# A deformable bottleneck and a batch-normalised bottleneck: table rows of two neighbours instead of four, and the last statistics taken from the product itself

## The chip, the cores and the metric

The kernel runs on one core of a Trainium2 chip. The metric is the device time of one execution in microseconds (us), on the only core used. Matrix products run on PE, its weight loads are shown as PEld; DVE, ACT and POOL are the vector, scalar and GpSimd engines; SP issues transfers. ACT and POOL issue transfers too, in the same order in which they do their other work.

## The reference, cut to what matters

Two layers follow each other on x of 4 images, 1024 channels, 56 x 56 pixels, all in float32. CB is 256.

```python
# layer 0
r = relu(conv1x1(x, w1) + b1)                      # 1024 -> 256
off = conv3x3(r, w_off) + b_off                    # 2 offsets for each of 9 taps and pixel
ys, xs = pixel + tap + off
y0, x0 = floor(ys), floor(xs); wy1, wx1 = ys - y0, xs - x0
sampled = ( r[y0, x0]     * (1-wy1)*(1-wx1) + r[y0, x0 + 1]     * (1-wy1)*wx1
          + r[y0 + 1, x0] * wy1*(1-wx1)     + r[y0 + 1, x0 + 1] * wy1*wx1 )   # 0 outside the image
r = relu(einsum('nckhw,ock->nohw', sampled, w2) + b2)
x1 = relu(x + conv1x1(r, w3) + b3)                 # 256 -> 1024
# layer 1
o = relu(bn(conv1x1(x1, w1) + b1))                 # bn: mean and variance over images and pixels
o = relu(bn(conv3x3(o, w2) + b2))
o = bn(conv1x1(o, w3) + b3)                        # 256 -> 1024
out = relu(x1 + softplus(residual_scale) * o)
```

Every bn needs the mean and the variance of a whole product, over all 4 x 3136 pixels, before one value of it can be scaled.

## The kernel before

Channels lie on the 128 partitions, so 1024 channels are 8 groups (KC) and 256 are 2 (KB). Pixels are worked in blocks of 8 image rows, 448 pixels: 7 blocks (NJ) an image, 28 in all. A float32 product of 128 x 448 is issued to PE as two instructions.

**The deformable layer.** stage_a (one block of an image) loads x (SP, L207), makes the 1x1 product (L211), ReLU to feat (ACT, L220), the offset product (L230), and turns feat by PE transposes (L254) into rows of one pixel each, ft (ACT, L260 to L263). ACT then writes ft to a table in device memory, one table for each image (L267, L271). A table row stands for one pixel of the image with a border of zeros, 58 pixels to a row (PW). It holds 256 channels for each of four neighbours: the pixel, its right neighbour, the one below, and the one below right. So every block is written four times, each time shifted, with two DMAs (384 KB and 80 KB): eight in all. The border is written with zeros at the start (L189). stage_b makes four weights for each pixel and tap and the row to read (L297 to L319).

stage_c takes a block of the image before. For each of the 9 taps, sampled fetches 4 tiles of 112 pixels: POOL gathers 112 table rows of 4 KB (L332) into one of 8 buffers g, ACT scales the first neighbour (L340), DVE adds the other three (L342), PE turns the sum (L351), and ACT copies two finished halves to sts (L357). The products with w2 (L369) run one tap behind. Then come ReLU (L385), the product with w3 (L408), the sum with x (DVE, L415), ReLU (L418), the store of x1 to device memory (L422), and layer 1's first product (L391) with its statistics (L426, L429).

What sets the order: the outer loop calls stage_a of image n, stage_b of the block before and stage_c of image n - 1, for each j. So the first 7 blocks have only stage_a, the last 7 only stage_c. Each engine works in the order of its own instruction list; a tile scheduler fixes that list when the program is built, from the program's order and its own estimate of times. On ACT the eight table writes of stage_a stand directly ahead of the two copies to sts with which the next block of stage_c begins (L357).

**Layer 1.** c2w and c3w are loaded, the first bn is applied on the way into padded images (L494), the 3x3 convolution runs (L515), its result stays in SBUF as y2, with its statistics (L524, L525).

**The last statistics.** The last product is z = c3w x y2, of 1024 channels. Its mean follows from the mean of y2, and its variance from the second moments of y2, a 256 x 256 matrix. So y2 is normalised (ACT, L594), turned to pixel rows by PE (L564), a reference value of each channel is subtracted (DVE, L578), POOL sets a column of ones (L571), and PE multiplies each chunk of 128 pixels with itself (moments, L583). At the end gram x c3w (L641), a product with c3w element by element (L644) and sums over channels on PE (L651) give mean and variance (L658 to L661), and scale_shift_of gives scale and shift.

**The last product.** Function wide makes one 128 x 448 piece of z in one of 4 PSUM banks (L533). DVE scales it and adds x1 (L675), ACT does shift and ReLU (L683), and the result is stored (L686). x1 comes back from device memory into 4 buffers x1f (SP, L672).

Of the kernel before, what the change touches and what calls it, by code (L numbers as in the profile page):

```python
# [8 lines left out]
F32 = mybir.dt.float32  # L9
I32 = mybir.dt.int32  # L10
AF = mybir.ActivationFunctionType
ALU = mybir.AluOpType

N, CIN, H, W = 4, 1024, 56, 56
CB = 256
# [31 lines left out]
def deform_bottleneck_then_bn_bottleneck(  # L47
# [30 lines left out]

    tables = [
        dram.tile([TROWS, 4, CB], F32, tag=f"table{n}", name=f"table{n}") for n in range(N)  # L80
# [18 lines left out]
    y2_stats = const.tile([128, KB, NB, 6], F32, tag="y2_stats", name="y2_stats")  # L99

    def scale_shift(stats, k, g, be, name):

        mv = const.tile([128, k, 2], F32, tag=f"mv_{name}", name=f"mv_{name}")
        for i in range(k):
            nc.vector.bn_aggr(mv[:, i, :], stats[:, i, :, :].rearrange("p b s -> p (b s)"))
        return scale_shift_of(mv[:, :, 0], mv[:, :, 1], k, g, be, name)

    def scale_shift_of(mean, var, k, g, be, name, bias=None):

        sc = const.tile([128, k], F32, tag=f"sc_{name}", name=f"sc_{name}")  # L110
        sh = const.tile([128, k], F32, tag=f"sh_{name}", name=f"sh_{name}")
        nc.scalar.activation(sc, var, AF.Sqrt, bias=eps_t)
        nc.vector.reciprocal(sc, sc)
        nc.vector.tensor_mul(sc, sc, g)
        if bias is None:
            nc.vector.tensor_mul(sh, mean, sc)
            nc.vector.tensor_sub(sh, be, sh)
        else:
            nc.vector.tensor_add(sh, mean, bias)
            nc.vector.tensor_sub(sh, bias, sh)  # L120
            nc.vector.tensor_mul(sh, sh, sc)
            nc.vector.tensor_add(sh, sh, be)
        return sc, sh


    with ExitStack() as l0:
# [57 lines left out]
        for n in range(N):  # L184
            for corner, s in enumerate((0, 1, PW, PW + 1)):
# [15 lines left out]
        def stage_a(n, j):  # L201
# [63 lines left out]
            for corner, s in enumerate((0, 1, PW, PW + 1)):  # L265
# [9 lines left out]
        def stage_b(n, j):  # L275
# [37 lines left out]
            for corner in range(4):  # L313
                wy, wx = (hi if corner // 2 else lo), (hi if corner % 2 else lo)
# [228 lines left out]


    stat = ctx.enter_context(tc.tile_pool(name="stat", bufs=1))
    gram = stat.tile([128, KB, KB, 128], F32, tag="gram", name="gram")
    dev = stat.tile([128, KB], F32, tag="dev", name="dev")
    ref = stat.tile([128, KB], F32, tag="ref", name="ref")
    ref_all = stat.tile([128, CB], F32, tag="ref_all", name="ref_all")
    part = stat.tile([128, 128], F32, tag="part", name="part")  # L550
    nc.vector.memset(part, 1.0 / 128)
    prod = stat.tile([128, KB, CIN], F32, tag="prod", name="prod")
    mom = stat.tile([128, 3, KC], F32, tag="mom", name="mom")
    chunks = [(n, at, min(128, HW - at)) for n in range(N) for at in range(0, HW, 128)]
    with ExitStack() as l2:
        pixp = l2.enter_context(tc.tile_pool(name="pixels", bufs=3))
        acc_g = ps2.tile([128, KB, 512], F32, tag="acc", name="acc_g")

        def pixels(i):

            tp = ps1.tile([128, 2, CB], F32, tag="bank", name=f"tp_{i}")
            for c, (n, at, m) in enumerate(chunks[i : i + 2]):
                for h in range(KB):
                    nc.tensor.transpose(  # L564
                        tp[:m, c, h * 128 : (h + 1) * 128], y2[n][:, h, at : at + m], ident
                    )
            yt = pixp.tile([128, 2, CB + 1], F32, tag="ytp", name=f"ytp_{i}")
            return tp, yt

        def centred(i, tp, yt):  # L570
            nc.gpsimd.memset(yt[:, :, CB : CB + 1], 1.0)  # L571
            ms = [m for _, _, m in chunks[i : i + 2]]
            for c in range(2) if min(ms) < 128 else (slice(0, 2),):
                m = ms[c] if isinstance(c, int) else 128
                of = ref_all if isinstance(c, int) else (
                    ref_all.rearrange("p (o c) -> p o c", o=1).to_broadcast([128, 2, CB])
                )
                nc.vector.tensor_tensor(yt[:m, c, :CB], tp[:m, c, :], of[:m], ALU.subtract)  # L578

        def moments(i, yt):  # L580
            for c, (n, at, m) in enumerate(chunks[i : i + 2]):
                for h in range(KB):
                    nc.tensor.matmul(  # L583
                        acc_g[:, h, : CB + 1 - h * 128],
                        yt[:m, c, h * 128 : (h + 1) * 128],
                        yt[:m, c, h * 128 :],
                        start=(i == 0 and c == 0),
                        stop=(i + c == len(chunks) - 1),
                    )

        def relu(n, j):
# [5 lines left out]

        done = 0
        before = None
        for i in range(0, len(chunks), 2):  # L600
            n, at, m = chunks[i + 1]
            while done * BLK < n * HW + at + m:
                relu(done // NJ, done % NJ)
                done += 1
            tp, yt = pixels(i)
            if i == 0:
                nc.vector.tensor_copy(yt[:, 0, :CB], tp[:, 0, :])
                first = ps1.tile([128, 512], F32, tag="bank", name="first")
                nc.tensor.matmul(first[:, :CB], part, yt[:, 0, :CB], start=True, stop=True)
                nc.vector.tensor_copy(ref_all, first[:, :CB])  # L610
                first_c = ps1.tile([128, 512], F32, tag="bank", name="first_c")
                for h in range(KB):
                    nc.tensor.matmul(
                        first_c[:, h : h + 1],
                        yt[:, 0, h * 128 : (h + 1) * 128],
                        part[:, 0:1],
                        start=True,
                        stop=True,
                    )
                nc.vector.tensor_copy(ref, first_c[:, :KB])  # L620
            centred(i, tp, yt)
            if before is not None:
                moments(*before)
            before = (i, yt)
        moments(*before)

        total = float(N * HW)
        nc.vector.tensor_scalar_mul(gram[:, 0], acc_g[:, 0, :CB].rearrange("p (b c) -> p b c", c=128), 1.0 / total)
        nc.vector.tensor_scalar_mul(gram[:, 1, 1], acc_g[:, 1, :128], 1.0 / total)
        nc.vector.tensor_scalar_mul(dev[:, 0:1], acc_g[:, 0, CB : CB + 1], 1.0 / total)  # L630
        nc.vector.tensor_scalar_mul(dev[:, 1:2], acc_g[:, 1, 128:129], 1.0 / total)
        nc.vector.tensor_add(ref, ref, dev)
        mirror = ps1.tile([128, 512], F32, tag="bank", name="mirror")
        nc.tensor.transpose(mirror[:, :128], gram[:, 0, 1], ident)
        nc.vector.tensor_copy(gram[:, 1, 0], mirror[:, :128])
        for h in range(KB):
            for half in range(2):
                pg = ps1.tile([128, 512], F32, tag="bank", name=f"pg_{h}_{half}")
                cs = slice(half * 512, (half + 1) * 512)
                for g in range(KB):  # L640
                    nc.tensor.matmul(  # L641
                        pg, gram[:, g, h], c3w[:, g, cs], start=(g == 0), stop=(g == KB - 1)
                    )
                nc.vector.tensor_mul(prod[:, h, cs], pg, c3w[:, h, cs])  # L644
        pm3 = ps1.tile([128, 3, KC], F32, tag="bank", name="pm3")
        nc.vector.memset(part[:, 0:1], 1.0)
        for k in range(KC):
            ks = slice(k * 128, (k + 1) * 128)
            for what, (of, by) in enumerate(((c3w, ref), (c3w, dev), (prod, None))):
                for h in range(KB):  # L650
                    nc.tensor.matmul(  # L651
                        pm3[:, what, k : k + 1],
                        of[:, h, ks],
                        part[:, 0:1] if by is None else by[:, h : h + 1],
                        start=(h == 0),
                        stop=(h == KB - 1),
                    )
        nc.vector.tensor_copy(mom, pm3)  # L658
        nc.vector.tensor_mul(mom[:, 1], mom[:, 1], mom[:, 1])
        nc.vector.tensor_sub(mom[:, 2], mom[:, 2], mom[:, 1])  # L660
        nc.vector.tensor_scalar_max(mom[:, 2], mom[:, 2], 0.0)  # L661
    sc3, sh3 = scale_shift_of(
        mom[:, 0], mom[:, 2], KC, cols("g3", KC), cols("be3", KC), "bn3", bias=cols("b3", KC)
    )
# [75 lines left out]
```

## Time and profile before

| | |
|---|---|
| time, median of 3 runs | 4442.2 us (4433.05 to 4461.87) |
| the profiled execution | 4433.05 us, of which the span is 4431.3 us |
| mean granted PE clock | 0.927 |
| PE busy | 3732.4 us (84%) |
| weight loads | 1918.2 us (43%) |
| DVE busy | 1907.6 us (43%) |
| ACT busy | 1237.1 us (28%) |
| POOL busy | 1119.7 us (25%) |
| gathers L332 | 1008, from issue to landing 10.4 us (median) |
| last gather issued | 3140.9 us |
| 3x3 convolution L515 | from 3203.5 us, for 759.6 us |
| first transpose of the moments L564 | 3968.5 us |
| last product L533 | 896 instructions, the first at 4078.2 us, the last at 4424.5 us |
| read from device memory, written | 638.65 MB, 169.79 MB |

How to read the profile: the span runs from the first to the last instruction of the profiled execution. Busy shares are means over stages of a very different kind, so most of what follows reads stretches of the span instead. In a time-ordered line the columns are start, duration, engine, line, operation, output and input with their shapes, count, and in brackets the idle time of the engine just before, with what ended it. An engine's name with a q (ACTq, SPq) marks the issuing of a transfer. A wait is listed as engine, tile and line, then what it waited for, total time, times, and the longest.

### The profile page before, as it was taken

The page shows a single profiled execution, that of the slowest core. Times are in us where ns is not written, and L with a number is a line of the kernel's source. Part 1 is how long each engine was busy: PE and PEld are TensorE (multiplying, and loading weights), DVE is VectorE, ACT ScalarE, POOL GpSimd, SP SyncE. Part 2 cuts the span into 40 slices and gives each one's busy share as a digit, 9 for nine tenths or more (in the row PEclk, how much of TensorE's full clock was granted, in tenths as well). Part 3 has the DMA queues.
Part 4 walks back from the last instruction along what each step waited for, and adds up shares of the span by engine and source line. Part 5 has one row for each costly group of instructions (what it writes and reads, how often), then busy time and mean ns, then how long its engine had stood idle before and what let it go on. Part 6 is the DMA issues. An engine that isn't in the chain of part 4 may idle for free. (4 is left out here: it accounts for less than half of the span.)

```text
span 4431.3 us, 35493 instructions
## 1 busy us (share of the span) xinstructions
PE 3732.4 (84%) x11135; PEld 1918.2 (43%) x11135; DVE 1907.6 (43%) x4208; ACT 1237.1 (28%) x2390; POOL 1119.7 (25%) x1067
## 2 busy tenths in 40 slices
PE   7887887778878878778887777787699999999999
PEld 3443344334443434333443333343355555558554
DVE  1355555545555545555555565655500000013444
ACT  0133333233332333333333333333310000021444
POOL 0233333333333333333333344443200000000000
PEclk9899998889998989999899889899899999999999
DMA  6787788888777887777877778888610000000998
GB/s 204 226 222 214 215 212 221 218 219 221 221 221 209 229 206 222 221 216 221 217 221 212 204 212 221 234 230 225 196 51 17 13 0 0 0 17 9 306 303 296
DMA packets 357149, 810.82 MB, mean 183 GB/s; under 512 B 30128, under 2 KB 243040, under 8 KB 356448
## 3 DMA queue, kind: packets, MB, share of 16 engines
q0 software_dynamic: 129024, 462.49, 40.7%
q1 hardware_dynamic: 102864, 176.25, 13.4%
q10 hardware_dynamic: 125072, 169.82, 10.9%
q8 instruction: 88, 1.44, 0.1%
q14 instruction: 101, 0.83, 0.1%
HBM read 638.65 MB, written 169.79 MB: 182 GB/s over the span
## 5 line engine op out<-in xcount | busy, mean ns | idle before, releaser
L332 POOL DMA_INDIRECT g<-table,idxs x1008 | 1112.4, 1104 | 2026.4 <-DVE s L342 1507.2
L342 DVE SCALAR_TENSOR_TENSOR s<-g,wts,s 112x256 f32<-112x256 f32 x3024 | 1364.9, 483 | 506.5 <-ACT s L340 454.2
L369 PE MATMUL acc<-sts,w 128*128 128x448 f32 x2016 | 1080.5, 656 | 404.8 <-ACT sts L357 404.8
L515 PE MATMUL acc<-pad,c2w 128*128 128x448 f32 x2016 | 759.5, 539 | 19.4 <-ACT pad L494 19.4
L340 ACT ACTIVATE s<-g,wts 112x256 f32<-112x256 f32 x1008 | 500.2, 509 | 923.5 <-DMA g<-table,idxs 671.5
L369 PEld LDWEIGHTS acc<-sts,w 128*128 128x128 f32 x2016 | 399.6, 226 | 643.8 <-ACT sts L357 483.9
L515 PEld LDWEIGHTS acc<-pad,c2w 128*128 128x128 f32 x2016 | 381.4, 189 | 397.5 <-issue 397.5
L351 PEld LDWEIGHTS stp<-ident,s 112*128 112x128 f32 x2016 | 269.0, 155 | 553.9 <-DVE s L342 344.6
L351 PE MATMUL stp<-ident,s 112*128 112x112 f32 x2016 | 369.9, 286 | 163.4 <-DVE s L342 157.7
L391 PE MATMUL acc<-x1t,c1w 128*128 128x448 f32 x896 | 381.1, 552 | 32.0 <-ACT x1t L418 31.9
L408 PE MATMUL pr<-r,w 128*128 128x448 f32 x896 | 376.5, 548 | 20.5 <-ACT r L385 20.5
L211 PE MATMUL acc<-xt,w 128*128 128x448 f32 x896 | 349.3, 547 | 29.6 <-DMA xt<-in_x_dram 29.6
L415 DVE SCALAR_TENSOR_TENSOR x1t<-pr,ch,xr 128x448 f32<-128x448 f32 x224 | 151.4, 682 | 458.2 <-PE pr L408 322.6
L533 PE MATMUL pf<-y,c3w 128*128 128x448 f32 x896 | 339.5, 542 | 0.0
L525 DVE BATCH_NORM_STATS2 y_stats<-y 128x6 f32<-128x448 f32 x56 | 32.3, 618 | 691.0 <-ACT y L524 691.0
L357 ACT COPY sts<-stp 128x448 f32<-128x448 f32 x504 | 243.0, 532 | 203.3 <-DMA table<-ft 107.0
L418 ACT ACTIVATE x1t<-x1t 128x448 f32<-128x448 f32 x224 | 129.1, 576 | 528.8 <-DVE x1t L415 502.7
L391 PEld LDWEIGHTS acc<-x1t,c1w 128*128 128x128 f32 x896 | 166.8, 191 | 214.7 <-issue 147.2
L408 PEld LDWEIGHTS pr<-r,w 128*128 128x128 f32 x896 | 170.9, 193 | 202.3 <-issue 133.7
L211 PEld LDWEIGHTS acc<-xt,w 128*128 128x128 f32 x896 | 170.9, 192 | 194.0 <-issue 184.7
L533 PEld LDWEIGHTS pf<-y,c3w 128*128 128x128 f32 x896 | 171.0, 191 | 166.5 <-issue 143.6
L242 DVE COPY offc<-pm 32x448 f32<-32x448 f32 (+1 forms) x84 | 51.4, 612 | 440.4 <-PE pm L230 439.6
(120 smaller groups left out, 1281.7 us busy)
## 6 DMA issues: line engine op xcount, KB each, us to landing
xt<-in_x_dram SPq DMA_DIRECT2D x112, 448.0 KB
xr<-in_x_dram SPq DMA_DIRECT2D x112, 448.0 KB
x_d<-x1t ACTq DMA_DIRECT2D x112, 448.0 KB
x1f<-x_d SPq DMA_DIRECT2D x112, 448.0 KB
out_dram<-x1f ACTq DMA_DIRECT2D x112, 448.0 KB
table<-ft ACTq DMA_DIRECT2D x112, 384.0 KB
g<-table,idxs POOLq DMA_INDIRECT x1008, 10.4
y_d<-y ACTq DMA_DIRECT2D x28, 448.0 KB
```

The source lines that it names most:

```text
L211: nc.tensor.matmul(acc[:, h, :BLK], w1[:, k, h * 128 : (h + 1) * 128], xt[:, d, :], start=(k == 0), stop=(k == KC - 1),)
L332: nc.gpsimd.indirect_dma_start(out=g, out_offset=None, in_=tables[n].rearrange("r q c -> r (q c)"), in_offset=bass.IndirectOffsetOnAxis(ap ...
L340: nc.scalar.activation(s, g[:, 0:CB], AF.Copy, scale=wt[:, 0])
L342: nc.vector.scalar_tensor_tensor(s, g[:, corner * CB : (corner + 1) * CB], wt[:, corner], s, ALU.mult, ALU.add,)
L351: nc.tensor.transpose(banks[h][:, t * PIX : (t + 1) * PIX], s[:, h * 128 : (h + 1) * 128], ident[:PIX, :PIX],)
L357: nc.scalar.copy(sts[:, h, :], banks[h])
L369: nc.tensor.matmul(acc[:, o, :BLK], w2[:, h, k, o * 128 : (o + 1) * 128], sts[:, h, :], start=(k == 0 and h == 0), stop=(k == TAPS - 1 and ...
L391: nc.tensor.matmul(acc3[:, h, :BLK], c1w[:, k, h * 128 : (h + 1) * 128], x1t, start=(k == 0), stop=(k == KC - 1),)
L408: nc.tensor.matmul(pr, w3[:, h, k * 128 : (k + 1) * 128], r2[:, h, :], start=(h == 0), stop=(h == KB - 1),)
L415: nc.vector.scalar_tensor_tensor(x1t[:, d, :], pr, col("a_b3", k), xr[:, d, :], ALU.add, ALU.add)
L515: nc.tensor.matmul(acc[:, o, :BLK], c2w[:, h, t, o * 128 : (o + 1) * 128], pads[n % 2][:, h, r0 : r0 + ROWS, kj : kj + W], start=(h == 0 a ...
L533: nc.tensor.matmul(pz, c3w[:, h, k * 128 : (k + 1) * 128], y2[n][:, h, j * BLK : (j + 1) * BLK], start=(h == 0), stop=(h == KB - 1),)
```

## The change

It has two parts.

Tables: a row holds two neighbours, the pixel and the one below, so it is 2 KB instead of 4 KB. The gather still fetches 4 KB for each pixel: a row and the next one, which is that of the right neighbour. The four values arrive as pixel, below, right, below right, so the weights of the second and third are exchanged. A block is written twice instead of four times, with four DMAs instead of eight; the border takes 12 DMAs instead of 24.

Statistics: the moments, their pool and their tiles are gone. In their place the whole last product is computed once more ahead of time, only for its statistics: for each block y2 is normalised, and bn_stats reads each of the 8 pieces from PSUM. scale_shift aggregates them (8 channel groups of 28 blocks) and takes over the branch with a bias.

```diff
     tables = [
-        dram.tile([TROWS, 4, CB], F32, tag=f"table{n}", name=f"table{n}") for n in range(N)
+        dram.tile([TROWS, 2, CB], F32, tag=f"table{n}", name=f"table{n}") for n in range(N)
     ]
...
+    z_stats = const.tile([128, KC, NB, 6], F32, tag="z_stats", name="z_stats")
+
+    def scale_shift(stats, k, g, be, name, bias=None):
-    def scale_shift(stats, k, g, be, name):
         mv = const.tile([128, k, 2], F32, tag=f"mv_{name}", name=f"mv_{name}")
         for i in range(k):
             nc.vector.bn_aggr(mv[:, i, :], stats[:, i, :, :].rearrange("p b s -> p (b s)"))
-        return scale_shift_of(mv[:, :, 0], mv[:, :, 1], k, g, be, name)
-
-    def scale_shift_of(mean, var, k, g, be, name, bias=None):
+        mean, var = mv[:, :, 0], mv[:, :, 1]
...
-            for corner, s in enumerate((0, 1, PW, PW + 1)):
+            for corner, s in enumerate((0, PW)):
                 first_row = PW - s + TPAD
...
-            for corner, s in enumerate((0, 1, PW, PW + 1)):
+            for corner, s in enumerate((0, PW)):
                 r = q - s + TPAD
...
-                wy, wx = (hi if corner // 2 else lo), (hi if corner % 2 else lo)
+                wy, wx = (hi if corner % 2 else lo), (hi if corner // 2 else lo)
...
-    stat = ctx.enter_context(tc.tile_pool(name="stat", bufs=1))
...
-        for i in range(0, len(chunks), 2):
-            n, at, m = chunks[i + 1]
-            while done * BLK < n * HW + at + m:
-                relu(done // NJ, done % NJ)
-                done += 1
-            tp, yt = pixels(i)
...
-            centred(i, tp, yt)
-            if before is not None:
-                moments(*before)
-            before = (i, yt)
-        moments(*before)
...
-    sc3, sh3 = scale_shift_of(
-        mom[:, 0], mom[:, 2], KC, cols("g3", KC), cols("be3", KC), "bn3", bias=cols("b3", KC)
+    for n in range(N):
+        for j in range(NJ):
             for h in range(KB):
                 ys = y2[n][:, h, j * BLK : (j + 1) * BLK]
                 nc.scalar.activation(
                     ys, ys, AF.Relu, bias=sh2[:, h : h + 1], scale=sc2[:, h : h + 1]
                 )
+            for k in range(KC):
+                nc.vector.bn_stats(z_stats[:, k, n * NJ + j, :], wide(n, j, k, "pz"))
+    sc3, sh3 = scale_shift(
+        z_stats, KC, cols("g3", KC), cols("be3", KC), "bn3", bias=cols("b3", KC)
     )
```

The gather itself, which no line of the diff shows, asks for a g tile of 4 x CB values from the table seen as rows of 2 x CB.

More of the change, by code (lines that the diff above doesn't have):

```diff
@@ L540, in wide @@
         return pz
-    stat = ctx.enter_context(tc.tile_pool(name="stat", bufs=1))
[L546 to L591, printed above, removed]
@@ L596, in relu @@
                 )
-        done = 0
-        before = None
-        for i in range(0, len(chunks), 2):
-            n, at, m = chunks[i + 1]
-            while done * BLK < n * HW + at + m:
-                relu(done // NJ, done % NJ)
-                done += 1
-            tp, yt = pixels(i)
[L606 to L620, printed above, removed]
-            centred(i, tp, yt)
-            if before is not None:
-                moments(*before)
-            before = (i, yt)
@@ L625, in deform_bottleneck_then_bn_bottleneck @@
-        moments(*before)
[L627 to L661, printed above, removed]
-    sc3, sh3 = scale_shift_of(
-        mom[:, 0], mom[:, 2], KC, cols("g3", KC), cols("be3", KC), "bn3", bias=cols("b3", KC)
+            for k in range(KC):
+                nc.vector.bn_stats(z_stats[:, k, n * NJ + j, :], wide(n, j, k, "pz"))
+    sc3, sh3 = scale_shift(
+        z_stats, KC, cols("g3", KC), cols("be3", KC), "bn3", bias=cols("b3", KC)
```

## The prediction

> **What bounds the kernel now.** I read four views of the profile, in this order. First the span in 40 slices, to find the stages:
>
> ```profile
> PE   7887887778878878778887777787699999999999
> DVE  1355555545555545555555565655500000013444
> DMA  6787788888777887777877778888610000000998
> GB/s 204 226 222 214 215 212 221 218 219 221 221 221 209 229 206 222 221 216 221 217 221 212 204 212 221 234 230 225 196 51 17 13 0 0 0 17 9 306 303 296
> ```
>
> A slice is 110.8 us. Up to about 3195 us (slice 29) no engine is full: PE 70 to 80%, DVE about 55%, DMA about 80%. That is the deformable layer, blocks of gathers. After it PE alone is full. Second, busy time by stretches of the late part:
>
> ```profile
> 3195.00:3968.00 773.00, 759.55 (x2016) 381.42 (x2016) 47.67 (x78) 77.17 (x119) 0.17 (x3) 0.99 0.05 17
> 3968.00:4062.80 94.80, 93.10 (x608) 85.61 (x609) 36.53 (x62) 36.28 (x56) 4.78 (x47) 0.97 0.02 7
> 4062.80:4088.00 25.20, 25.20 (x116) 20.55 (x115) 3.17 (x7) 0.00 (x0) 0.00 (x0) 0.71 0.00 1
> 4088.00:4431.00 343.00, 337.40 (x894) 170.19 (x894) 150.18 (x236) 145.91 (x225) 0.00 (x0) 0.99 0.89 295
> ```
>
> Columns: length, then busy time and count of PE, weight loads, DVE, ACT and POOL, granted clock, DMA share, GB/s. The 3x3 convolution, the statistics (second and third row: what the change removes) and the last product follow one another with PE full, the products at a clock of 0.99. What PE gains or loses there is span. Third, the chain of work, which gives PE's true rate, since the durations of pipelined matmuls overlap:
>
> ```profile
> 3203.47 759.56 PE acc L515 x2016
> 4087.91 325.48 PE pf L533 x862
> ```
>
> 759.56/2016 = 0.3768 us and 325.48/862 = 0.3776 us for each of the two instructions that one 128x448 product becomes. Fourth, time-ordered lines of ACT and POOL around a block's start, and the waits:
>
> ```profile
> 1099.68 0.38 ACT L263 COPY ft<-ftp 80x256 f32<-80x256 f32 x1
> 1099.83 0.37 ACTq L267 DMA_DIRECT2D table<-ft  x1
> 1100.29 0.44 ACTq L271 DMA_DIRECT2D table<-ft  x1
> ...
> 1104.78 0.54 ACTq L271 DMA_DIRECT2D table<-ft  x1
> 1105.36 0.97 ACT L357 COPY sts<-stp 128x448 f32<-128x448 f32 x2 [5.30 <-DMA table<-ft]
> ```
>
> ```profile
> 1058.88 0.93 POOL L332 DMA_INDIRECT g<-table,idxs  x1 [1.95 <-ACT x1t L418]
> 1109.59 1.23 POOL L332 DMA_INDIRECT g<-table,idxs  x1 [49.78 <-DVE s L342]
> 1111.13 6.42 POOL L332 DMA_INDIRECT g<-table,idxs  x1 [0.31 <-DVE s L342]
> ```
>
> ```profile
> ACT sts L357 <- DMA table<-ft: 107.0, 21, 9.7
> ```
>
> A block (about 112 us) has two halves. For some 62 us (59 to 66 by POOL's lines of all blocks) 36 gathers run, most of the time with the DMA engines full (share 1.03 from 1010 to 1070) at 1.73 us a gather. Then POOL stands for 50 us: all 8 g buffers are full, and PE does the 1x1 products and the next image's first products. That half ends only when ACT has issued eight table writes and at last copies sts: 5.3 us of waiting, 107.0 us in the 21 blocks that have such writes.
>
> [...]
>
> **The change, part by part.**
>
> Removed, the moments: PE's first transpose at 3968.49 to the last product of pm (L651) at 4087.78, 119.3 us, in which one pf product (2 x 0.378 = 0.8 us) was already done: 118.5 us.
>
> Added, the product twice: 4 images x 7 blocks x 8 output groups x 2 = 448 products, 896 instructions x 0.3776 = 338.3 us, and 0.6 us at its start, because ACT normalises the second half of y2 0.64 us after the first (first transposes at 3968.49 and 3969.13). 338.9 us. What runs beside it: two Relu of 0.746 us per 12.1 us on ACT, and 224 bn_stats from PSUM. The trace has bn_stats only from SBUF (L525, 618 ns);[...] an estimate of 0.68 us, as the scalar_tensor_tensor from PSUM (L675, 682 ns). Bounds: 0.62 and, a tenth above L675, 0.75. Against 1.51 us of PE per output group all of these hide behind PE, 4 banks deep; uncovered they would be 152 us.
>
> Its end: in DVE's order each bn_aggr of the last block stands behind its own bn_stats, so one aggregate (875 ns) and 1.9 us for root, reciprocal and scales follow the last statistics: 0.68 + 0.88 + 1.9 + the first STT's 0.68 = 4.1 us. PE meanwhile fills four banks with pf, 4 x 1.51 = 6.0 us: no stall. Statistics: 338.9 - 118.5 = **+220.4 us**.
>
> The x1f loads are issued when the convolution ends, and only four fit: nothing changes for them.
>
> Table writes: per block of stage_a 4 DMAs in place of 8 on ACT's queue, and 0.95 MB instead of 1.9 MB (26.6 MB less in all). The rows of L267 and L271 give 4.96 to 5.10 us from the first issue to the last's end in 18 of the 20 blocks behind the first, and 2.07 to 2.12 us for the first four: 2.9 us less on ACT, the end of which releases sts, taps, the next ACT scalings, DVE and POOL's first gather. The product that sts copies is there at about 1101.0, the fourth issue ends near 1101.9: ACT is still last, so the whole 2.9 us counts. 20 x 2.9 = 58 us. In the first block the eight take 9.87 us, four 1.93; the transpose (195.95) is then last and 7 us come off. Sum **-65 us**.
>
> The bytes: they go out in POOL's pause. In blocks of the last image, with no table writes, the first gather (2737.61) also lands 12.0 us later (ACT at 2749.64), as at 1109.59 to 1121.59. So writes have drained when gathers start; fewer bytes are worth 0, at most 1 us a block (20 us).
>
> Zero borders: 12 issues instead of 24, at the very start. They hold ACT to 42.26 us, but PE then waits for xt until 39.64 and does six matmuls before it needs feat: 0, at most 5 us.
>
> The gathers: same 1008 instructions, same 4 KB per row (in order: pixel, the one below, then both for the right neighbour; swapped weights cost nothing). The trace of before has no read at 2 KB pitch, where neighbouring rows share half their bytes. Spacing there ranges from 1.44 to 1.95 us by block[...]. I take no change, bounds of -4% and +4% on 28 x 62 = 1740 us: 70 us either way. If a row became two packets, the upper end.
>
> Orders: PE issues the four products of the first tap in one go instead of two by two, as it does already in the last image: nothing.
>
> Sum: 4431.3 + 220.4 - 65 = 4586.7 us of span, 1.8 us around it: 4588.5, against 4433.05 of the profiled execution. That run is the fastest of the three; the median lies 9 us above. I put 4593, halfway.
>
> **The rivals.** (a) The ACT time saved is given back: gathers start 2.9 us sooner, but the DMA engines or DVE take it up. For it: the gather half is DMA-bound. Against: its length hardly depends on when it starts (62 us with the long pause, 63 without stage_a). 4593 + 65 = 4658.
> (b) The new rows gather worse: two packets, or two engines on the same bytes at once. For it: gathers reach 265 GB/s where xt loads reached 413 (30 to 35 us). 5% of 1740 us: 4680.
> (c) Not slower: shared rows make memory easier, and gathers run down to DVE's three passes, 3 x 0.483 = 1.45 us. Four blocks already show 1.44 to 1.49. Over the 26 steady gathers of the other 24 blocks: 0.28 x 26 x 24 = 175 us, 4418. It decides from 0.15 us a gather on all 28 blocks (109 us), where the time comes within 1% of before. Against: the engines show a share of 1.03 throughout, and bytes per gather are the same.
> (d) Half of (c), 4510.
>
> **How the numbers follow.** Forecast 0.64, (a) 0.10, (b) 0.14, (c) 0.05, (d) 0.07. The forecast's own range is 4560 to 4625; to hold 8 in 10 it reaches towards (a) and (d): 4530 to 4660. About 1% is what a measurement can tell from no change. Only (c), with stronger gains than its sum, is faster; (c) and a strong (d) are within 1%: 0.02 and 0.04; slower 0.94.
>
> **What would show it.** Right: 896 pz instructions in 338 us with DVE about 45% busy; pf without a pause behind them; the wait of sts on table writes near 45 us instead of 107; gather spacing as before; blocks some 2.9 us shorter. Wrong: a gather packet count that doubles, spacing off by more than 0.1 us, PE waiting on bn_stats, or a lower clock in 1440 us of dense PE.

## The result and the profile after

The kernel after takes 4578.3 us (median of 4 runs, 4572.8 to 4602.5), the kernel before, on the same chip, 4446.4 us (4 runs, 4433.1 to 4461.9): a ratio of 1.031 with a 95% interval of 1.026 to 1.036. Slower, by 132 us. The forecast was 4593.

The profiled execution of after took 4572.81 us, its span is 4571.0 us: 139.7 us more than the 4431.3 us of before. On both sides it is the fastest execution. First the span in slices, of 114.3 us now:

```profile
PE   8888777888888888887787777778999999999999
DVE  1555555555555555555556656661000000444444
```

The deformable layer ends in slice 27. The slices in which PE is full are now twelve, and in the last six of them DVE is at four tenths: three slices of the new pass, three of the last product. The chain of work that ended last (start, length, what) and the stretch of the new pass (columns as in the prediction) give lengths and loads:

```profile
3122.42 760.66 PE acc L515 x2016
...
3888.53 338.86 PE pz L533 x896
4227.39 318.72 PE pf L533 x848
```

```profile
3885.00:4229.00 344.00, 340.47 (x901) 172.09 (x902) 150.43 (x238) 37.46 (x58) 0.00 (x0) 0.99 0.01 5
```

The pass takes 338.86 us at a granted clock of 0.99, with DVE busy 150 of 344 us. The convolution starts 81.05 us earlier than before (3203.47). What stands between the two kernels, by groups of instructions (busy and mean ns, then the idle time ahead of them and what ended it):

```profile
L533 PE MATMUL pz<-y,c3w 128*128 128x448 f32 x896 | 338.9, 541 | 5.5 <-ACT y L547 5.5
L533 PE MATMUL pf<-y,c3w 128*128 128x448 f32 x896 | 336.9, 539 | 0.0
L551 DVE BATCH_NORM_STATS2 z_stats<-pz 128x6 f32<-128x448 f32 x224 | 141.5, 632 | 192.8 <-PE pz L533 192.8
L357 ACT COPY sts<-stp 128x448 f32<-128x448 f32 x504 | 243.2, 532 | 161.6 <-PE stp L351 149.6 <-issue 5.8 <-DMA table<-ft 4.8
```

PE never waits for bn_stats in pz, and pf has no pause in front of it. DVE waits for PE instead (192.8 us). The wait of sts on table writes, 107.0 us before, is 4.8 and that on PE's transposes has grown from 94.9 to 149.6. Part of this is a change of name only, as the start of one block of after shows. ACT and then POOL at the start of one block of after:

```profile
955.05 0.38 ACT L263 COPY ft<-ftp 80x256 f32<-80x256 f32 x1
955.19 0.37 ACTq L267 DMA_DIRECT2D table<-ft  x1
...
956.62 0.56 ACTq L271 DMA_DIRECT2D table<-ft  x1
957.22 0.97 ACT L357 COPY sts<-stp 128x448 f32<-128x448 f32 x2 [1.80 <-issue]
```

```profile
961.45 1.23 POOL L332 DMA_INDIRECT g<-table,idxs  x1 [46.31 <-DVE s L342]
```

Four issues take 1.99 us (955.19 to 957.18), where eight took about 5. sts starts 0.04 us behind the last of them, so it still waits for them, 1.80 us here and in most of the blocks. Behind the first block that holds in 17 of 20 blocks; in the other three the transposes end last. The profile names PE for it in 16 of the 20, and "issue" or the table write in the others, because the transposes end only about 1 us earlier. And POOL's idle time is 46.3 us, where the block shown of before had 49.8. The queues (packets, MB, share), before and then after:

```profile
q0 software_dynamic: 129024, 462.49, 40.7%
...
q10 hardware_dynamic: 125072, 169.82, 10.9%
```

```profile
q0 software_dynamic: 129024, 462.49, 38.9%
...
q10 hardware_dynamic: 96808, 142.72, 8.6%
```

q0, the gathers, has exactly the packets and bytes of before: with overlapping 4 KB reads they are 129024 packets as with rows of their own. q10 holds the table writes.

Where the 139.7 us come from, and what the prediction had for each (profiled executions, us; a pause runs from a block's last gather to the next block's first; "the first pf" is the one from which the pf products run on without a break):

| | before | after | difference | predicted |
|---|---|---|---|---|
| first gather issued | 177.2 | 156.3 | -20.9 | 0 to -5 |
| first block's 48 gathers | 89.7 | 82.1 | -7.6 | -7 |
| 20 pauses with table writes, mean | 50.47 | 47.54 | 20 x -2.93 = -58.6 | -58 |
| 7 other pauses, mean | 28.82 | 27.47 | 7 x -1.35 = -9.4 | 0 |
| gathers of blocks 1 to 20, mean | 62.16 | 63.17 | 20 x 1.01 = +20.2 | 0, bounds 70 |
| the rest up to the convolution (6 blocks and the last) | | | -4.7 | 0 |
| convolution starts | 3203.5 | 3122.4 | -81.0 | -65 |
| convolution L515 | 759.6 | 760.7 | +1.1 | 0 |
| its end to the first pf | 124.9 | 344.3 | +219.4 | +220.4 |
| first pf to the end | 343.4 | 343.6 | +0.2 | 0 |

The first row was the surprise. ACT's lines at the very start, before and then after:

```profile
1.19 40.99 ACTq L189 DMA_DIRECT2D table<-zero  x24
42.26 1.28 ACT L220 ACT_TABLE_LOAD   x1 [42.26 <-DMA table<-zero]
```

```profile
1.19 16.28 ACTq L189 DMA_DIRECT2D table<-zero  x12
17.56 1.28 ACT L220 ACT_TABLE_LOAD   x1 [17.56 <-DMA table<-zero]
```

and PE's, before and after:

```profile
17.52 8.42 PE L211 MATMUL acc<-xt,w 128*128 128x448 f32 x16 [17.52 <-DMA xt<-in_x_dram]
27.18 6.28 PE L211 MATMUL acc<-xt,w 128*128 128x448 f32 x16 [1.24 <-DMA xt<-in_x_dram]
39.64 4.85 PE L211 MATMUL acc<-xt,w 128*128 128x448 f32 x6 [6.18 <-DMA xt<-in_x_dram]
```

```profile
19.95 17.02 PE L211 MATMUL acc<-xt,w 128*128 128x448 f32 x38 [19.95 <-DMA xt<-in_x_dram]
```

In before PE has to wait for xt again and again while the zero writes are out; in after it waits once. Up to 180 us these waits come to 29.6 us in before and 19.9 in after, so they hold about half of the 20.9 us; how the rest comes about was not followed. The prediction read these two facts side by side (ACT held to 42 us, PE late for xt) and took them for independent.

### The profile page after: what moved, and what is told of

Its sections match the earlier page's. It is cut to its first block, busy times and chain, and to the rows that moved or that the text cites. A ratio compares the mean times of both kernels' runs of the same rounds, so it can differ in the third digit from the quotient of the medians.

```text
span 4571.0 us, 35698 instructions
## 1 busy us (share of the span) xinstructions
PE 3944.2 (86%) x11312; PEld 1983.0 (43%) x11312; DVE 2013.2 (44%) x4367; ACT 1236.9 (27%) x2390; POOL 1140.7 (25%) x1017
## 3 DMA queue, kind: packets, MB, share of 16 engines
q0 software_dynamic: 129024, 462.49, 38.9%
## 5 line engine op out<-in xcount | busy, mean ns | idle before, releaser
L332 POOL DMA_INDIRECT g<-table,idxs x1008 | 1138.3, 1129 | 1921.5 <-DVE s L342 1422.3
L515 PE MATMUL acc<-pad,c2w 128*128 128x448 f32 x2016 | 760.6, 539 | 19.1 <-ACT pad L494 19.1
L515 PEld LDWEIGHTS acc<-pad,c2w 128*128 128x128 f32 x2016 | 381.8, 189 | 397.9 <-issue 397.7
L211 PE MATMUL acc<-xt,w 128*128 128x448 f32 x896 | 345.7, 543 | 19.9 <-DMA xt<-in_x_dram 19.9
L525 DVE BATCH_NORM_STATS2 y_stats<-y 128x6 f32<-128x448 f32 x56 | 32.3, 618 | 718.2 <-ACT y L524 718.2
L533 PE MATMUL pz<-y,c3w 128*128 128x448 f32 x896 | 338.9, 541 | 5.5 <-ACT y L547 5.5
L357 ACT COPY sts<-stp 128x448 f32<-128x448 f32 x504 | 243.2, 532 | 161.6 <-PE stp L351 149.6
L533 PEld LDWEIGHTS pz<-y,c3w 128*128 128x128 f32 x896 | 171.0, 191 | 173.4 <-issue 166.6
```

The lines of the kernel that those rows point to most:

```text
L211: nc.tensor.matmul(acc[:, h, :BLK], w1[:, k, h * 128 : (h + 1) * 128], xt[:, d, :], start=(k == 0), stop=(k == KC - 1),)
L332: nc.gpsimd.indirect_dma_start(out=g, out_offset=None, in_=tables[n].rearrange("r q c -> r (q c)"), in_offset=bass.IndirectOffsetOnAxis(ap ...
L357: nc.scalar.copy(sts[:, h, :], banks[h])
L515: nc.tensor.matmul(acc[:, o, :BLK], c2w[:, h, t, o * 128 : (o + 1) * 128], pads[n % 2][:, h, r0 : r0 + ROWS, kj : kj + W], start=(h == 0 a ...
L533: nc.tensor.matmul(pz, c3w[:, h, k * 128 : (k + 1) * 128], y2[n][:, h, j * BLK : (j + 1) * BLK], start=(h == 0), stop=(h == KB - 1),)
```

## The experiments

Twelve runs, each set beside runs of the kernel before on the same chip.

**The two parts alone.** stats_alone is after with the tables of before; tables_alone is before with this edit:

```diff
-        dram.tile([TROWS, 4, CB], ...
+        dram.tile([TROWS, 2, CB], ...
-            for corner, s in enumerate((0, 1, PW, PW + 1)):      # L185 and L265
+            for corner, s in enumerate((0, PW)):
-                wy, wx = (hi if corner // 2 else lo), (hi if corner % 2 else lo)
+                wy, wx = (hi if corner % 2 else lo), (hi if corner // 2 else lo)
```

> Only the statistics are changed; the table keeps four neighbours. If the two parts add up, as the sum of the prediction takes it, this costs 219 us: about 4446 + 219 = 4665 us, the first product of the convolution starts near 3203 us as before, and the pz stage lasts 339 us. If the two parts help or hinder each other (for example through a clock that falls in the longer dense stretch), it differs from that by more than 15 us.

> Only the tables are changed; the moments stay. Theory: -81 us, as between the two starts of the convolution (3203.5 and 3122.4), of which 21 us before the first gather, 8 us in the first block, and some 50 us from 20 pauses that are 3 us shorter, less what the gathers vary: about 4365 us. Rival: gathers of overlapping rows are slower or faster in themselves: then the 28 gather halves differ from 62.4 us in the mean by more than 1.5 us. A version that is faster than both kernels if the theory holds.

Measured: tables_alone 4388.0 us, ratio 0.988 (0.980 to 0.995), -63 us; first gather 156.4, pauses 48.01, gathers of a block 62.98 and the convolution at 3138.7. That is the table part as predicted (-65), though by other terms: the pauses gave 49 of the 58 us, the start 21 where 0 to 5 stood. The -81 of its own expectation is missed by 18 us; the interval, about -88 to -22 us, holds both. stats_alone 4621.7 us, ratio 1.041 (1.036 to 1.045): +171, not +219. In its profile the pass is as long as in after, and the missing time lies ahead of the convolution, which starts at 3135.4 although nothing of that part was edited. (The profiled execution is the fastest of its four, 31 us under their median, so 68 us is too much for a typical one.) The sum of the parts, 108 us, is 24 less than the 132 us of the whole. The statistics are taken up again below.

**What the zero writes did.** before_zero64 is before with zero writes of 64 rows, 24 as before, with more bytes (rows beyond the border are overwritten later by the tables' own writes):

```diff
-        zero = wp.tile([PW + 2, CB], ...
+        zero = wp.tile([64, CB], ...
+                        r0, r1 = (0, 64) if r0 == 0 else (TROWS - 64, TROWS)
```

> The kernel before, with each zero write widened from 59, 58 or 1 row to 64 rows (rows of the image that it covers are written over later). Theory: the start is held by zero writes that run on one or two of the 16 DMA engines[...]. Then the 24 issues end near 8 us instead of 42, the first xt no longer wait, and the first gather comes 20 to 28 us earlier, with more bytes and as many issues: about 4423 us. Rival: the number of issues or the bytes hold the start: no gain, or a loss of some us.

Measured: 4425.7 us, 0.996 (0.994 to 0.998), first gather at 159.2 instead of 177.2. Twice as many issues as after and more bytes, yet nearly all of after's earlier start. In the profiled execution only 7 of these 18 us are left when the convolution starts (3196.7): the gathers take longer (94.7 us in the first block, 89.7 in before). ACT's line at the start of before_zero64:

```profile
1.19 18.00 ACTq L190 DMA_DIRECT2D table<-zero  x24
```

The mean busy share of the DMA engines in 40 slices of the first 45 us, before and then before_zero64:

```profile
DMA  0149931162149771000189611999999700011110
```

```profile
DMA  0178999787999798968999999999999999726999
```

No run here shows the DMA engines one by one, but the shares fit zero writes that keep very few of them busy. By the times of its own packets q10, the queue of the zero writes, took 5.9% of the time of 16 engines from 1.19 to 42.18 us in before, which is 0.94 of one engine's time, an estimate from that share. From 18.0 to 21.4 us q10 takes 6.3%, all else 1.1%, and the share of both is 0.07 at 27 GB/s; from 36.0 to 39.5 us, where PE stands idle because an xt load has not landed, it is 0.06 at 23 GB/s. In before_zero64 no slice from 2.25 to 39.4 us is under six tenths, with as many issues and 1536 KB instead of 944. So the one or two engines of the expectation fit before; that the number of rows sets how many was the author's assumption and was not shown. After has four of each of these writes instead of eight; before_zero64 shows that the start it gains needs no change of the tables.

**ACT's issuing or the bytes.** before_sp is before with `nc.sync` in place of `nc.scalar` at L267 and L271. tables_eight is tables_alone with each of the four writes cut in two:

```diff
+                for t0, t1 in ((0, 1), (1, QFULL)):
                     nc.scalar.dma_start(
-                    tables[n][r : r + QFULL * 128, ...], ft[:, :QFULL, :]
+                    tables[n][r + t0 * 128 : r + t1 * 128, ...], ft[:, t0:t1, :]
...
+                for p0, p1 in ((0, 48), (48, QREST)):
```

> The kernel before, with the table writes issued by SP instead of ACT: the same eight DMAs and bytes. Theory: what the table change saves in each block is ACT's time to issue, so here the copy to sts comes about 4 us earlier than before (transposes are then last), and 21 blocks give 80 to 90 us: about 4360 us. Rival: the bytes of the table writes hold the gathers: no gain. Between them: gathers start earlier but into writes that are still under way, and half of it is lost.

> The new tables with the statistics of before, and each of the four table writes of a block cut in two, so that eight are issued again with half the bytes. Theory that the issuing on ACT is what the blocks gained: the eight take near 5 us again, a pause lasts near 50.5 us as before, and only the earlier start (21 us) is left of the gain of tables_alone: near 4425. Rival, that the bytes are: a pause stays near 48 us and the time near that of tables_alone, 4388.

Measured: before_sp 4323.4 us, 0.972 (0.968 to 0.975): -127.6 with all eight writes and all bytes, twice the gain of tables_alone and more than the 80 to 90 us of the expectation. Two views of one of its blocks, ACT and SP:

```profile
1055.51 0.38 ACT L263 COPY ft<-ftp 80x256 f32<-80x256 f32 x1
1056.14 0.53 ACT L357 COPY sts<-stp 128x448 f32<-128x448 f32 x1 [0.25 <-PE stp L351]
```

```profile
1055.65 0.37 SPq L267 DMA_DIRECT2D table<-ft  x1
...
1060.09 0.52 SPq L271 DMA_DIRECT2D table<-ft  x1
```

The same issues take 5.0 us on SP, and sts no longer waits for them: it starts 0.25 us after ft, where in before it waited 4.8 to 5.4. tables_eight gave 4377.2 us, 0.985 (0.980 to 0.990), on the side of the bytes rather than of the issues. But it had not doubled ACT's issue time: the eight smaller issues took 3.48 us a block, not 5, and by its interval it is not told from tables_alone, so it does not decide. Put in order of the time that ACT spends on issues per block (sum of their durations over 28), the pauses follow it:

| | bytes | issues | ACT issuing, us a block | mean pause |
|---|---|---|---|---|
| before | all | 8 | 4.98 | 50.47 |
| stats_again (below) | all | 8 | 4.30 | 49.37 |
| tables_eight | half | 8 | 3.48 | 48.88 |
| tables_alone | half | 4 | 1.97 | 48.01 |
| after | half | 4 | 1.86 | 47.54 |
| before_sp | all | 8 | 0 | 44.58 |
| tables_zero64_sp (below) | half | 4 | 0 | 44.71 |

The last two rows settle it for the pause: with the issues off ACT, half the bytes are worth nothing (44.71 against 44.58). The last kernel has the wider zero writes too; the new tables with SP and nothing else were not run. 5.9 us of the pause went with 5.0 us of issuing. Not all of the 5.9 is shown to be ACT's: the seven pauses without table writes are 1.2 us shorter in before_sp too (28.82 and 27.63), and why was not found.

**DVE in the new pass.** stats_twice is after with each of its bn_stats done twice from the same bank:

```diff
-                nc.vector.bn_stats(z_stats[:, k, n * NJ + j, :], wide(n, j, k, "pz"))
+                pz = wide(n, j, k, "pz")
+                nc.vector.bn_stats(z_twice[:, k, n * NJ + j, :], pz)
+                nc.vector.bn_stats(z_stats[:, k, n * NJ + j, :], pz)
```

> The kernel after with every bn_stats of the last product done twice from the same PSUM bank. Theory that PE alone sets the length of the new pass: 2 x 0.632 = 1.26 us of DVE for a group stays under the 1.51 us of PE, nothing is added but one bn_stats at the end (under 2 us), near 4580. Rival, that DVE's reading of the banks holds PE: any wait of PE for DVE shows, and the pass grows by up to 141 us, to 4720 at most.

Measured: 4574.8 us, 1.030 (1.025 to 1.036), after's own ratio.

```profile
L534 PE MATMUL pz<-y,c3w 128*128 128x448 f32 x896 | 338.6, 541 | 5.5 <-ACT y L548 5.5
L534 PE MATMUL pf<-y,c3w 128*128 128x448 f32 x896 | 337.4, 539 | 1.3 <-DVE x1f L568 1.3
L553 DVE BATCH_NORM_STATS2 z_twice<-pz 128x6 f32<-128x448 f32 x224 | 141.0, 630 | 77.9 <-PE pz L534 77.9
```

137 us more of DVE's work cost PE nothing in pz and 1.3 us at its end. PE sets the length of the pass, with 1.24 us of DVE's work beside 1.51 us of PE's for a group.

**Both savings at once.** tables_zero64_sp has tables_alone's edit, before_zero64's and before_sp's.

> The new tables with the statistics of before, the zero writes of 64 rows instead of 58 or 59, and the table writes issued from SP instead of ACT. If the three savings come from one resource, ACT's time in issuing, they do not add up: near 4300, that is before_sp (4323) less the earlier start (some 20 us), and nothing for two instead of four copies of a block. If the bytes or the number of writes count by themselves, it goes to near 4255, that is 63 us more below before_sp.

Measured: 4315.3 us, 0.971 (0.967 to 0.976), the ratio of before_sp and 15 us above the lower gain of the expectation. The savings don't add up. The first gather comes 28 us earlier than before_sp's (148.3 against 176.3), but the first block's gathers then take 88.7 instead of 78.2, and the convolution starts only 11 us earlier.

**Why the statistics cost 171 and not 219.** before_shift is before with one unused tile where after has z_stats:

```diff
+    unused = const.tile([128, KC, NB, 6], F32, ...)
+    nc.vector.memset(unused, 0.0)
```

> The kernel before with one unused constant tile of 128 x 1344 float32 (5.4 KB a partition, set to zero once) where the new statistics have z_stats, so that everything allocated after it in SBUF lies as in the kernel after; nothing else changes. Theory that the place in SBUF is what shortened the gather part of stats_alone: the convolution starts some 50 to 68 us earlier, near 3140 us, and the time is near 4400. Rival, that stats_alone differed for another reason (its executions spread from 4591 to 4638): the time stays within 10 of the kernel before, near 4450, and the convolution starts near 3203.

Measured: 4444.7 us, 1.000 (0.997 to 1.002), convolution at 3213.3. The place in SBUF is not it. Then the kernel of stats_alone once more (stats_again), and before with the new pass beside its moments (the same loop with bn_stats, ahead of L664's scale_shift_of):

> The same kernel as stats_alone, placed on the chip anew. If what shortened its gather part (convolution at 3135 us instead of 3203) was chance of that run, it now takes the kernel before plus 219, near 4660, with the convolution near 3203 and eight table writes issued in 4.65 us. If it belongs to the program, it takes near 4620 again, with the eight issued in 4.00 us.

> The kernel before, with its moments, and the new pass with its bn_stats after them, whose statistics are not used. The work up to the convolution is that of the kernel before. If removing the moments is what shortens the gather part, this kernel has none of it: the convolution starts near 3203 us, eight table writes are issued in 4.65 us, and the time is the kernel before plus the pass of 339: near 4785. If having the new pass is what shortens it, the convolution starts near 3140 us and the time is near 4735.

Measured: stats_again 4639.3 us against 4468.3, 1.040 (1.036 to 1.044), the ratio of stats_alone; convolution at 3179.4. pass_and_moments 4800.8 us, 1.077 (1.071 to 1.082), +332, convolution at 3235.0. So the shortening is not chance and goes with taking the moments out. Its size varies: the same kernel's convolution started at 3135.4 and at 3179.4. ACT's issues showed one part of a way: in a block of stats_again

```profile
985.08 0.46 ACTq L267 DMA_DIRECT2D table<-ft  x1
...
986.16 0.45 ACTq L267 DMA_DIRECT2D table<-ft  x1
```

the third and fifth issue take 0.46 and 0.45 us, where in a block of before the same two take 0.57 and 0.81:

```profile
990.73 0.57 ACTq L267 DMA_DIRECT2D table<-ft  x1
...
991.91 0.81 ACTq L267 DMA_DIRECT2D table<-ft  x1
```

Every kernel with the moments whose writes are not cut in two shows the longer ones in nearly every block, every kernel without them the shorter. The eight issues of a block have a median of 4.00 us (stats_alone) instead of 4.65; the means of the table above are higher by a few long ones. Whether that is the way was the last question, put with the issues moved to SP:

> stats_alone with its eight table writes issued from SP, to be set beside before_sp (0.972 of the kernel before, 4323). If the new statistics shorten the gather part by way of ACT's issuing (4.00 instead of 4.65 us a block), the shortening is gone here and the full 220 shows: near 4543, 1.021 of the kernel before, with the convolution near 3089 as in before_sp. If they shorten it in another way, some 49 us are still missing: near 4494, 1.010, with the convolution near 3040.

> The kernel after with zero writes of 64 rows and the table writes issued from SP, to be set beside tables_zero64_sp (0.971 of the kernel before, 4315). By way of ACT's issuing: near 4535, 1.020 of the kernel before, the convolution near 3078. In another way: near 4486, 1.009, the convolution near 3030.

Measured: stats_sp 4496.8 us, 1.012 (1.009 to 1.016), after_zero64_sp 4478.8 us, 1.009 (1.005 to 1.012). Their convolutions:

```profile
3046.48 760.15 PE acc L515 x2016
```

```profile
3029.26 759.54 PE acc L516 x2016
```

Both on the second theory: the shortening stays with ACT's issuing out of the way, and pauses are as in the partners (44.47 and 44.28). Most of it is in the gathers here: 61.51 us a block (before_sp 63.36) and 61.94 (tables_zero64_sp 63.56). That is no general rule: after has 63.17 us against 62.98 of tables_alone, and the kernels with the moments and the old tables lie between 62.16 (before) and 64.26 (pass_and_moments). The four pairs that differ in the statistics alone:

| new statistics, moments | ratios to before | difference | convolution starts |
|---|---|---|---|
| stats_alone, before | 1.041, 1 | 0.041 | 3135.4, 3203.5 |
| after, tables_alone | 1.031, 0.988 | 0.043 | 3122.4, 3138.7 |
| stats_sp, before_sp | 1.012, 0.972 | 0.041 | 3046.5, 3088.9 |
| after_zero64_sp, tables_zero64_sp | 1.009, 0.971 | 0.037 | 3029.3, 3077.6 |

0.037 to 0.043 of 4446 us is 166 to 191 us, against 219 on the path (0.049). So 28 to 53 us are missing, by the medians. In three of the pairs the convolution starts 42 to 68 us earlier, in work whose instructions are not edited. In the pair of after it is 16 us, a further 8 us lie behind the convolution, where tables_alone takes 476.2 us and before 468.2, and by the intervals its 0.043 can't be told from 0.049. What connects the moments with the work ahead of them was not found; the cause stays open.

## Why the prediction was right, and where it was not

The time, 4578 against 4593, and the reason for it held: the new pass is on PE's path at PE's pace, and the table part gives back a part of it.

- **Statistics, +220.4.** Measured +219.4 on the path, and doubling DVE's work does not lengthen it (stats_twice). bn_stats was sized at 0.68 us and takes 0.632, which changes nothing under 1.51 us of PE. What the step left out is that without the code of the moments the kernel is 28 to 53 us shorter elsewhere; no part of the working could have given that.
- **Table writes, -65.** The 20 pauses gave -58.6 for the 58 foreseen, the first block -7.6 for 7. Some luck is in the 58.6: tables_alone, with the table edit by itself, gave 49, and seven pauses without table writes became 1.35 us shorter unforeseen. That it is the issuing was shown by before_sp, and that half the bytes are worth 0 in a pause by tables_zero64_sp. That sts would still wait near 45 us for the issues holds in part (about 1.8 us in 17 of 20 blocks and 2.2 in the first, some 33 us) but not by the profile's name for it, 4.8 us: issues and transposes end within 1 us, as the step's own two times (1101.0 and 1101.9) had it.
- **Zero borders, "0, at most 5 us".** This is the term that was mis-sized: -20.9 in the trace, and 18 us of it come with zero writes of 64 rows alone (before_zero64). The step reasoned that PE waits for xt until 39.64 anyway, so ACT's 42.26 is no bound. That reading was right, but the xt loads were late because of the same zero writes: with zero writes of 64 rows (before_zero64) PE's first 38 matmuls are done at 34.0 us instead of 44.5. The cause of the cover was the thing that the change cut in half.
- **Gathers, unchanged.** From before to tables_alone they went from 62.16 to 62.98 us a block, in after to 63.17: within the bounds, and neither rival (b) (5%) nor (c) (16%) is there. before_zero64 and before_shift, with rows that don't overlap, take 62.91 and 62.90. q0's packets did not change either, so rows that overlap cost nothing that these runs can tell.
- **Rival (a), the ACT time is given back.** It is seen in small only: after's gathers are 20 us longer over 20 blocks, and tables_alone still gains 63 us. In before_zero64 and tables_zero64_sp it is what happens to most of the earlier start.
- **The sum** came out near also because errors of both signs met: 21 us of start and 9 us of other pauses not foreseen, against 20 us of longer gathers. That the whole came out 15 us under the forecast is in part luck.

The best kernels of these are the two with the moments kept and the table writes on SP, at 0.971 and 0.972 of before: tables_zero64_sp at 4315 us and before_sp, an edit of one word in two places, at 4323.

## What to carry to other kernels

Price a product that is computed once more by its instructions times their pace on the engine that is full, and then look only for waits at its seams; here DVE's work stayed hidden at 0.63 us and at 1.24 us beside 1.51 us of PE. When a wait covers a cost, ask whether the cost is what makes the wait: an edit that seemed hidden may move its own cover. And before halving the bytes of small writes, see on which in-order queue they are issued and who stands behind it; here moving them was worth twice as much as halving them (127.6 and 63 us).

## What the runs showed of the hardware

- 24 zero writes of 59, 58 and 1 rows (944 KB, before) held ACT's queue for 41.0 us; 24 of 64 rows (1536 KB, before_zero64) for 18.0 us.
- The third and fifth table-write issue of a block, of the same bytes, took 0.57 and 0.80 us (medians) in the kernels with the moments and 0.43 to 0.46 in those without, on ACT and on SP (before_sp, stats_sp); not explained.
- bn_stats on 448 values took 632 ns from PSUM (L551, after) and 618 from SBUF (L525, before and after): 14 ns apart. A second one on the same bank took 614 (stats_twice).
- Gathers of 4 KB that start every 2 KB ran as those on their own 4 KB rows: 63.0 and 62.2 us for 36 of 112 rows (tables_alone, before).
